# Layer 0's spectrum: Fourier and filter products issued ahead of the next band's mixing product

## The chip, the cores and the metric

The kernel runs on one core of a Trainium2 chip. The metric is device time in microseconds (us), the median of three runs. A core has engines that work through their own queues of instructions in order and meet only by waiting for one another: TensorE (PE in the profile; its weight loads are PEld) multiplies matrices into PSUM, VectorE (DVE), ScalarE (ACT) and GpSimd (POOL) work elementwise, and SyncE (SP) issues most transfers (DMA). TensorE's clock is not constant; the profile shows the share that was granted.

## What is computed

Eight images of 256 channels and 32 x 32 pixels pass two layers. Layer 0 is attention followed by a gated convolution network with a filter in the frequency domain; layer 1 is causal attention over 1024 tokens and a mixture of eight experts. The change is in layer 0, and there in the end of its second half (g1, g2: gammas):

```
x = x + g1 * attention(norm1(x))            # 4 heads, 1024 positions, depthwise 3x3 on v, projection
h = dwconv3(conv1x1(norm2(x), pi_w))        # 256 -> 1024 channels
h = gelu(h[:, :512]) * h[:, 512:]
y = conv1x1(h, po_w)                        # 512 -> 256: the "mixing product"
y = irfft2(rfft2(blocks_8x8(y)) * fft_p)    # filter on each 8x8 block
x = x + g2 * y
```

## The kernel before

**Tiling.** Channels or pixels lie on 128 partitions. An image is two tiles of 128 x 1024. In the spectrum (`spectrum(b)`, L1160) the image is cut into four bands of eight rows. Each band passes three steps. `first(n)` multiplies the band's hidden values with `pow_` (eight matmuls, tile `pz`) and ACT copies the result to `zf`. `second(z)` multiplies with the Fourier matrix (`pf`, one matmul) and VectorE multiplies the result with the filter (`gf`). `third(n, gf)` transforms back (`py`, four matmuls) and VectorE adds it to the image (`t<-py`, two instructions). After the last band the image is stored to `t_d`, and the image three places on is loaded into its buffer, both on SP's queue.

**Buffers.** `pz` comes from a PSUM pool that attention's scores `s` also use. `pf`, `py`, `ms`, `tpy`, `tr`, `rbn` and the projection's `pp` all come from another PSUM pool, `ps_m`, that has two buffers (tag `mm`): each new tile of these waits until whoever reads the buffer's last tile is done. `zf` and `gf` share three buffers in SBUF.

**Stages.** Layer 0 overlaps three images. In stage i (`main_of(i)`, L1240) image i is in attention; image i-1 gets its last projection half (`project`, L995) and its second norm (`norm2`, L1012); image i-2 is in the spectrum. Every step is a generator that is advanced by one yield at a time, and each engine executes its instructions in the order in which the program wrote them (`InOrder`, L61). So the nesting of the generators is the order of the queues. `silent` advances a generator without passing its yields on, `some` passes n of them, and `weave` alternates two generators (L1213 to L1230).

**Beside the main order**, `level` (L461) sets VectorE's convolution taps: after each yield of the main generator it issues taps (`v_conv`, L879: 16 taps `o<-vpad`, eight for each half of the channels; then `hidden`, L1063) until VectorE's planned time has reached the stage's share (`SHARE`) of TensorE's planned time. The planned times are fixed costs per instruction (`TensorCost`, L82; `vector_cost`, L101). The taps `o<-vpad` start from what ACT writes in `v_middle` (L873).

**The second norm** (`rms_norm`, L709) shares the stretch with the spectrum: ACT squares (`sq`), TensorE sums (`ms`), ACT scales (`yr`), TensorE turns (`tpy`), POOL computes seven small steps that end in `r`, TensorE turns back (`tr`), ACT copies (`rT`), TensorE spreads (`rbn`, twice) and VectorE writes `xn`. Between POOL's steps and `tr` stand five empty yields, so that other steps can be woven in.

After the eight stages an ending (L1340 to L1369) runs the spectra of images 6 and 7 beside the first token work of layer 1. For image 7 the mixing products are made ahead (`mix`, L1145), so there `first` is a copy alone.

Of the kernel before, what the change touches and what calls it, by code (L numbers as in the profile page):

```python
# [105 lines left out]
def conv_attn_hybrid_kernel(  # L106
# [34 lines left out]
    def col(name, i=0, n=1):  # L141
        o, w = _VOFF[name]
        assert i + n <= w
        if o >= NVEC0:
            return more[0][:, o - NVEC0 + i : o - NVEC0 + i + n]
        return vec[:, o + i : o + i + n]
# [431 lines left out]
    with ExitStack() as l0:  # L578
# [9 lines left out]
        def load_x(b):  # L588
            t[b] = two.tile([P, KC, N], F32, tag="t", name="t", bufs=3)
            nc.sync.dma_start(t[b], xv[b])  # L590
# [96 lines left out]
        def inside(p, r0, c0, h):  # L687
            o = r0 * (W + 1) + c0
            return p[:, o : o + h * (W + 1)].rearrange("p (h w) -> p h w", w=W + 1)[:, :, :W]
# [7 lines left out]
        def rows(ap):  # L697
            return ap.rearrange("p (h w) -> p h w", w=W)
# [174 lines left out]
        def v_middle(b):  # L873
            o = att[b]["o"] = one.tile([P, KC, N], F32, tag="o", name="o")
            for g in range(KC):
                mid = inside(vpad[g], 1, 1, H)
                act.activation(rows(o[:, g, :]), mid, AF.Identity, bias=pe_o[:, g : g + 1], scale=pe_w[:, g, 4:5])
# [112 lines left out]
        def finish(b):  # L990
            while att[b]["rest"]:
                att[b]["rest"].pop(0)()
                yield 0.4

        def project(b, halves):  # L995
            for h in halves:
                hs = slice(h * HALF, (h + 1) * HALF)
                if h == 0:
                    both = ps_s.tile([P, KC, HALF], F32, tag="s", name="pp")
                    pps = [both[:, g, :] for g in range(KC)]  # L1000
                else:
                    pps = [ps_m.tile([P, HALF], F32, tag="mm", name="pp") for _ in range(KC)]
                for g in range(KC):
                    conv1x1(pps[g], projw, g * P, att[b]["o"], hs)
                    yield 1.7
                for g in range(KC):
                    tb = t[b][:, g, hs]
                    dve.scalar_tensor_tensor(tb, pps[g], proj_o[:, g : g + 1], tb, ALU.add, ALU.add)
# [3 lines left out]
        def norm2(b, gaps=3):  # L1012
            xn2[b] = one.tile([P, KC, N], F32, tag="xn2", name="xn2")
            yield from rms_norm(b, "n2w", xn2[b], gaps)
            ready2[b] = True
# [120 lines left out]
        def gelu_steps(b):  # L1136
            hid = hid_of[b]
            while hid["gelu"] < ng:
                h1 = hid["h"][hid["gelu"]]
                act.activation(h1, h1, AF.Gelu)  # L1140
                hid["gelu"] += 1
                gate(b)
                yield 0.0
# [16 lines left out]
        def spectrum(b):  # L1160

            hid = hid_of[b]["out"]
            nb = H // PS

            def first(n):
                if b in mixed:
                    pz = mixed[b][n // 2][:, n % 2]
                    z = two.tile([P, 2, C], F32, tag="ev", name="zf", bufs=3)
                    act.copy(z, pz)
                    return z  # L1170
                pz = ps_s.tile([P, 2, C], F32, tag="s", name="pz")
                for k in range(2):
                    for g in range(ng):
                        blk = hid[g][:, (2 * n + k) * P : (2 * n + k + 1) * P]
                        pe.matmul(pz[:, k, :], blk, pow_[:, g, :], start=(g == 0), stop=(g == ng - 1))
                z = two.tile([P, 2, C], F32, tag="ev", name="zf", bufs=3)
                act.copy(z, pz)
                return z

            def second(z):  # L1180
                pf = ps_m.tile([P, 2, C], F32, tag="mm", name="pf")
                pe.matmul(pf, dft, z, start=True, stop=True)
                gf = two.tile([P, 2, C], F32, tag="ev", name="gf", bufs=3)
                dve.tensor_mul(gf, pf, filt.unsqueeze(1).to_broadcast([P, 2, C]))
                return gf

            def third(n, gf):
                py = ps_m.tile([P, KC, PS, 2, W // 2], F32, tag="mm", name="py")
                for g in range(KC):
                    for k in range(2):  # L1190
                        pe.matmul(py[:, g, :, k, :], gf[:, k, g * P : (g + 1) * P], idft, start=True, stop=True)
                for g in range(KC):
                    tb = t[b][:, g, n * BAND : (n + 1) * BAND]
                    dve.scalar_tensor_tensor(
                        tb, py[:, g].rearrange("p r k c -> p (r k c)"), col("gam2", g), tb, ALU.mult, ALU.add
                    )

            z, gf = {}, {}
            for n in range(nb + 2):
                if n < nb:  # L1200
                    z[n] = first(n)
                    yield 3.5
                if 1 <= n <= nb:
                    gf[n - 1] = second(z.pop(n - 1))
                    yield 0.9
                if n >= 2:
                    third(n - 2, gf.pop(n - 2))
                    yield 0.9
            nc.sync.dma_start(t_d[b], t[b])
            if b + 3 < B:  # L1210
                load_x(b + 3)

        def weave(main, side, every, rest=True):  # L1213

            for n, us in enumerate(main):
                yield us
                if n % every == every - 1:
                    step = next(side, None)
                    if step is not None:
                        yield step  # L1220
            if rest:
                yield from side

        def some(steps, n):
            for us in itertools.islice(steps, n):
                yield us

        def silent(steps, n=None):
            for _ in itertools.islice(steps, n):
                pass  # L1230

        def none():
            yield from ()

        def later_on(n, steps):
            for _ in range(n):
                yield 0.0
            yield from steps

        def main_of(i):  # L1240

            steps = attend(i)
            if i >= 1:
                if i == 1:
                    second = norm2(i - 1)
                    silent(steps, 1)
                    silent(project(i - 1, (1,)))  # L1250
                    silent(second, 2)
                    v_middle(i)
                    yield from weave(second, steps, 2, rest=False)
                else:
                    mixing, second = spectrum(i - 2), norm2(i - 1, 5)
                    silent(second, 1)
                    silent(mixing, 1)
                    silent(project(i - 1, (1,)))
                    silent(second, 1)
                    v_middle(i)  # L1260
                    yield from some(mixing, 1)
                    yield from some(second, 1)
                    yield from some(mixing, 1)
                    yield from weave(second, mixing, 1, rest=False)
                    yield from weave(mixing, steps, 2, rest=False)
            yield from weave(steps, later_on(3, queries_keys(i + 1)) if 1 <= i < B - 1 else none(), 1)
            gelus = gelu_steps(i - 1) if i >= 1 else none()
            if i + 1 < B:
                stack(i + 1)
                steps, ends = values(i + 1), finish(i)  # L1270
                yield from some(gelus, 2)
                yield from some(steps, 2)
                yield from gelus
                yield from some(ends, 1)
                yield from project(i, (0,))
                yield from some(steps, 2)
                yield from some(ends, 1)
                yield from some(steps, 1)
                yield from ends
                yield from steps  # L1280
            else:
                yield from gelus
                yield from some(finish(i), 1)
                yield from project(i, (0,))
# [62 lines left out]

        norm0, keys0 = first_tokens(early, bank0, bank0)
        mixing, second, ends = spectrum(B - 2), norm2(B - 1), finish(B - 1)
        silent(second, 1)  # L1350
        silent(mixing, 1)
# [718 lines left out]
```

## Time and profile before

| what | value |
|---|---|
| median of three runs | 3064.48 us (3064.29 to 3064.49) |
| the profiled execution's own time | 3065.18 us |
| its span, first to last instruction | 3063.5 us |
| mean granted TensorE clock | 0.979 |
| TensorE busy | 2913.9 us, 95% |
| VectorE busy | 2339.7 us, 76% |
| ScalarE busy | 1621.6 us, 53% |
| layer 0's stages i = 2 to 7, start of the first mixing product in i = 3, 4, 5, 6, 7 | 453.26, 607.12, 760.84, 914.06, 1067.91 us |
| 32 filter products `gf`, one | 685 ns |
| waits of TensorE and its weight loads for `gf` | 24.0 and 30.9 us |

The page of the profile shows one execution. Times of instructions count from the span's start. A row of a timeline gives start, duration, engine, operation, output and inputs with shapes, how many equal instructions it merges, and in brackets how long the engine was idle before it and whose end it waited for. A matmul's end is modelled, since matmuls are pipelined. Where a helper records the instructions, all carry its line (L73), so they are told apart by their tiles.

### The profile page before, as it was taken

Reading aid. Unit: us, or ns where it says so; the run is one execution under the profiler, and the core shown is the slowest. Engines: PE = TensorE matmul, PEld = TensorE weight load, DVE = VectorE, ACT = ScalarE, POOL = GpSimd, SP = SyncE. Lnnn points to the kernel's source line nnn. Section 1 sums busy time; section 2 is a strip of 40 time slices with the busy share of each in tenths; the row PEclk is TensorE's granted clock in tenths of the full one; section 3 lists DMA queues with packets and bytes.
Section 4 is the critical chain, followed back from the end, with each engine's and each line's share of the span. In section 5 each row is a group of like instructions: output and inputs, shape, how many; then the busy total and the mean of one; then the engine's idle time right before and its main releaser. Section 6 shows DMA issues by size and latency. Waiting matters only on the chain.

```text
span 3063.5 us, 41588 instructions
## 1 busy us (share of the span) xinstructions
PE 2913.9 (95%) x16802; PEld 1923.7 (63%) x16802; DVE 2339.7 (76%) x2886; ACT 1621.6 (53%) x2440; POOL 317.1 (10%) x453
## 2 busy tenths in 40 slices
PE   7989999999999989889999999999999999999998
PEld 4644655555555555456666666677777777777775
DVE  2378888888888878776566654688988988888887
ACT  2555554545454535434444443565666666666664
POOL 1011111111111110011222222000000000000000
PEclk8999999999999989999999999999999999999999
DMA  6203030303030301003333311421211251122210
GB/s 196 48 10 83 28 84 28 83 29 83 29 83 29 83 15 35 16 35 128 131 133 122 126 78 69 165 83 49 90 69 69 97 186 69 69 76 90 76 69 29
DMA packets 63856, 234.87 MB, mean 77 GB/s; under 512 B 5590, under 2 KB 13862, under 8 KB 54822
## 3 DMA queue, kind: packets, MB, share of 16 engines
q1 hardware_dynamic: 63654, 232.12, 23.1%
q8 instruction: 134, 2.20, 0.3%
q14 instruction: 68, 0.56, 0.1%
HBM read 140.61 MB, written 91.49 MB: 76 GB/s over the span
## 4 chain that ended last, share of the span: by engine, by line
PE 74%; DVE 14%; ACT 6%; POOL 2%; DMA 2%; issue 2%; SPq 0%; ACTq 0%; DVEq 0%; POOLq 0%
PE pm L73 12%; PE pa L73 11%; PE q L73 11%; PE po L73 9%; PE s L73 6%; PE ph L73 6%; PE pq L73 3%; DVE conv L73 3%; PE sums L73 3%; DVE o L73 3%; DVE x L73 2%; ACT zt_e L73 2%; PE pz L73 2%; PE pv L73 2%; PE pp L73 2%
## 5 line engine op out<-in xcount | busy, mean ns | idle before, releaser
L73 PE MATMUL pa<-ze,w 128*128 128x512 f32 x1488 | 423.2, 393 | 0.0
L73 DVE SCALAR_TENSOR_TENSOR x<-hpad,vec,x 128x1024 f32<-128x1024 f32 x248 | 316.8, 1283 | 68.4 <-ACT x L73 60.9
L73 DVE SCALAR_TENSOR_TENSOR conv<-hpad,vec,conv 128x1024 f32<-128x1024 f32 x256 | 327.4, 1283 | 9.7 <-ACT conv L73 3.6
L73 PEld LDWEIGHTS pa<-ze,w 128*128 128x128 f32 x1488 | 278.4, 188 | 63.3 <-issue 3.3
L73 ACT ACTIVATE h<-pa,bn_o,s1a 128x512 f32<-128x512 f32 x256 | 198.6, 776 | 202.1 <-PE pa L73 202.1
L73 ACT ACTIVATE pT<-s 128x1024 f32<-128x1024 f32 x256 | 247.6, 1024 | 84.4 <-PE s L73 84.3
L73 PE MATMUL po<-pT,vT 128*32 128x256 f32 x4096 | 271.9, 383 | 0.0
L73 PE MATMUL q<-h2p,w 128*128 128x512 f32 x768 | 270.1, 460 | 0.1
L73 DVE SCALAR_TENSOR_TENSOR h<-pa,s1b,h 128x512 f32<-128x512 f32 x256 | 191.6, 748 | 96.4 <-PE pa L73 87.7
L73 PE MATMUL ph<-xn,piw 128*128 128x512 f32 x512 | 238.9, 608 | 13.4 <-ACT vpad L73 6.9
L73 PE MATMUL pm<-h,w 128*128 128x512 f32 x512 | 242.0, 595 | 0.0
L73 PE MATMUL q<-z_first,w 128*128 128x512 f32 x768 | 216.0, 390 | 2.8 <-DVE z_first L73 1.7
L73 PE MATMUL pm<-h1p,w 128*128 128x512 f32 x768 | 216.1, 389 | 0.5 <-DVE h1p L73 0.5
L73 PEld LDWEIGHTS q<-h2p,w 128*128 128x128 f32 x768 | 144.8, 189 | 84.3 <-issue 60.1
L73 DVE SCALAR_TENSOR_TENSOR o<-vpad,pe_w,o 128x1024 f32<-128x1024 f32 x128 | 164.0, 1283 | 26.1 <-ACT o L73 22.9
L73 PE MATMUL s<-qst,kst 128*128 128x256 f32 x1024 | 172.2, 311 | 8.9 <-ACT pT L73 6.3
L73 PEld LDWEIGHTS po<-pT,vT 128*32 128x32 f32 x4096 | 120.1, 110 | 84.4 <-issue 2.8
L73 PEld LDWEIGHTS ph<-xn,piw 128*128 128x128 f32 x512 | 92.3, 192 | 127.5 <-issue 99.5
L73 PEld LDWEIGHTS q<-z_first,w 128*128 128x128 f32 x768 | 143.8, 188 | 34.1 <-DVE z_first L73 2.9
L73 PEld LDWEIGHTS s<-qst,kst 128*128 128x128 f32 x1024 | 136.3, 193 | 45.2 <-issue 28.8
L73 PEld LDWEIGHTS pm<-h1p,w 128*128 128x128 f32 x768 | 144.1, 188 | 31.6 <-DVE h1p L73 0.9
L73 PE MATMUL sums<-pT,ones 128*32 128x256 f32 x2048 | 157.6, 379 | 0.0
(281 smaller groups left out, 5105.8 us busy)
## 6 DMA issues: line engine op xcount, KB each, us to landing
ze<-zd SPq DMA_DIRECT2D x29, 1536.0 KB, 6.4
qst<-part SPq DMA_DIRECT2D x32, 512.0 KB, 9.5
kst<-part SPq DMA_DIRECT2D x32, 512.0 KB, 16.4
te<-ud SPq DMA_DIRECT2D x32, 512.0 KB, 4.1
wd<-parts_w SPq DMA_DIRECT2D x20, 768.0 KB, 3.7
w<-wd SPq DMA_DIRECT2D x20, 768.0 KB, 5.7
zd<-parts SPq DMA_DIRECT2D x14, 1024.0 KB, 3.8
ud<-te SPq DMA_DIRECT2D x18, 512.0 KB, 3.4
```

What stands on the lines that cost most here:

```text
L73: return self._tc.keep_in_program_order(method(*args, **kwargs))
```

## The change

Two edits. In the loop of `spectrum` the second step of band n-1 is issued ahead of the first step of band n, no longer behind it. In `main_of`, for stages i of 2 and up, one more step of the spectrum is issued at once behind the projection and the norm's second step (the `ms` of the first half): with the new order, that is the second step of band 0. The number of steps is the same, so each later step of the spectrum falls one place further on among the norm's steps.

```diff
             z, gf = {}, {}
             for n in range(nb + 2):
+                if 1 <= n <= nb:
+                    gf[n - 1] = second(z.pop(n - 1))
+                    yield 0.9
                 if n < nb:
                     z[n] = first(n)
                     yield 3.5
-                if 1 <= n <= nb:
-                    gf[n - 1] = second(z.pop(n - 1))
-                    yield 0.9
                 if n >= 2:
                     third(n - 2, gf.pop(n - 2))
                     yield 0.9
...
                     silent(mixing, 1)
                     silent(project(i - 1, (1,)))
                     silent(second, 1)
+                    silent(mixing, 1)
                     v_middle(i)
                     yield from some(mixing, 1)
                     yield from some(second, 1)
```

On the queues of TensorE and VectorE in stages 2 to 6 that gives (taps: `o<-vpad`; numbers are bands):

```
TensorE before  pz0 pp ms | pz1 ms pf0 tpy pz2 pf1 py0 pz3 pf2 py1 tr pf3 rbn py2 rbn py3 s
TensorE after   pz0 pp ms | pf0 pz1 ms pf1 tpy pz2 py0 pf2 pz3 py1 pf3 tr py2 rbn py3 rbn s
VectorE before  t<-pp | 8 taps gf0 3 taps gf1 t0 2 taps gf2 1 tap t1 gf3 xn t2 xn t3 2 taps
VectorE after   t<-pp | gf0 8 taps gf1 3 taps t0 gf2 3 taps t1 gf3 t2 xn t3 xn 2 taps
```

In stage 7 the taps are 9, 3, 3 and 1: before, ahead of gf0, gf1, gf2 (with t1 behind it) and gf3; after, ahead of gf1, t0, t1 and t2; none follow. In the ending, `pf0` moves ahead of `rb` and `pz1`, `pf1` ahead of `pp`, and `pz2` and `pz3` come later among the norm's and the tokens' steps (`ms`, `tpt`). ACT's order changes only in the ending.

## The prediction

> **What bounds it now.** I began with the page: busy shares and the clock row.
>
> ```profile
> PE 2913.9 (95%) x16802; PEld 1923.7 (63%) x16802; DVE 2339.7 (76%) x2886; ACT 1621.6 (53%) x2440; POOL 317.1 (10%) x453
> PEclk8999999999999989999999999999999999999999
> ```
>
> TensorE is the bound over the whole, and the chain of waits gives it 74%. The change touches one stretch of each image stage, so I went on to the timeline of TensorE in the stage that starts at 453.26 (i=3: image 1's spectrum runs beside image 2's second norm).
>
> ```profile
> 474.34 2.07 PE L73 MATMUL py<-idft,gf 128*128 128x128 f32 x8 [3.64 <-DVE gf L73]
> 476.20 5.46 PE L73 MATMUL pz<-pow__152,hid 128*128 128x256 f32 x16
> 483.39 0.38 PE L73 MATMUL tr<-ident,r 128*8 128x128 f32 x2
> 489.23 1.19 PE L73 MATMUL s<-qst,kst 128*128 128x256 f32 x8
> ```
>
> Start and duration are in front, the idle time before and its releaser in brackets. TensorE waits 3.64 us for the filter product of band 0, then runs slowly: the third mixing product 5.46 us, against 3.62 for the same one at 466.22. At 489.23 the next attention begins (s). VectorE in the same stretch:
>
> ```profile
> 463.15 10.53 DVE L73 SCALAR_TENSOR_TENSOR o<-vpad,pe_w,o 128x1024 f32<-128x1024 f32 x8 [2.05 <-ACT o L73]
> 473.60 0.68 DVE L73 TENSOR_TENSOR gf<-pf,filt 128x512 f32<-128x512 f32 x1
> 478.03 0.68 DVE L73 TENSOR_TENSOR gf<-pf,filt 128x512 f32<-128x512 f32 x1
> 482.56 0.69 DVE L73 TENSOR_TENSOR gf<-pf,filt 128x512 f32<-128x512 f32 x1 [0.54 <-PE pf L73]
> 500.51 19.65 DVE L73 SCALAR_TENSOR_TENSOR x<-hpad,vec,x 128x1024 f32<-128x1024 f32 x15 [7.61 <-ACT x L73]
> ```
>
> The first gf stands behind eight taps. From 463.15 to 490.3 VectorE has hardly a gap, so it, not the 3.64 us, sets when s starts. Stage i=5 proves it:
>
> ```profile
> 781.92 1.16 PE L73 MATMUL py<-idft,gf 128*128 128x128 f32 x8 [3.64 <-DVE gf L73]
> 782.91 3.62 PE L73 MATMUL pz<-pow__152,hid 128*128 128x256 f32 x16
> 796.18 1.20 PE L73 MATMUL s<-qst,kst 128*128 128x256 f32 x8
> ```
>
> The same wait, but no slow clock: py and pz are issued in 4.5 us, not 7.2, and yet s starts only 0.63 us earlier in its stage (35.34 us after the first pz, against 35.97). From s to the next stage's first pz it is 117.87, 117.88 and 117.87 us in three stages (642.97 to 760.84, 796.18 to 914.06, 950.04 to 1067.91). So a move of s is paid one for one, times six stages. VectorE's own lateness after s is free: it idles 7.61 us before 500.51.
>
> **The change, part by part.** No instruction is added or taken away, and no DMA is moved past another: store and load of t stay behind the last third step on SP's queue, and the last py pair ends about a microsecond earlier. I work on i=3's clock with start-to-start times: tap 1.31 (10.45/8), gf 0.60, t pair 0.79, xn pair 1.34, pz 3.45, py 0.9, pf 0.9; gf to its py 0.75; t to the next py 1.02.
>
> First, pf0 goes from 465.04 to behind ms. Its PSUM buffer is free when the second t<-pp is read (461.1), so it runs 461.2 to 462.2; gf0 runs at 462.3, in the 2.05 us in which VectorE waits for ACT's o. It costs nothing while that cover holds, to 463.15 (0.2 us to spare); without it up to 0.6 us, all taps behind it. That takes 0.60 us out of VectorE's full stretch. TensorE's pz1, ms1, tpy and pz2 all move back 1.0 to 1.3 us, inside what was idle time; pf1 waits about 0.3 us for zf1. ACT's yr and y move back as far, and POOL's 7.6 us chain for r ends near 475.6, well before tr.
>
> Second, py0 no longer waits: its gf is long there, so it runs at 471.0 to 471.9. But the wait isn't gone. In the built order gf1 now stands behind the eight taps (473.6), and pf2 uses the PSUM buffer that gf1 reads: pf2 waits to 474.35, 2.4 us instead of 3.64. Then pz3 to 478.7, py1 (after the t pair of 478.1) 479.1, pf3 480.0 to 480.9.
>
> Third, tr. It waited for gf2; now it takes the buffer of py1, so it waits for the second t pair, and between gf2 and that pair stand three taps, where it was two ahead of gf2 and one behind. VectorE: gf1 473.6, three taps, t0 478.1, gf2 478.9, three taps, t1 483.4, gf3 484.2. tr can't start before 484.3. That is a new wait of 3.4 us, with py2 (needs gf3), rbn, py3 and s queued behind it, each in turn waiting for VectorE. In the old order this tail was fed: tr stood at 483.39.
>
> What follows tr, I take from whole stretches. At full clock (i=5) tr to s is 790.34 to 796.18, 5.84 us; pf3 has left it (1.0), so 4.8, and s starts at 489.1. At half clock I use i=7:
>
> ```profile
> 1099.93 0.38 PE L73 MATMUL tr<-ident,r 128*8 128x128 f32 x2 [1.39 <-DVE gf L73]
> 1100.76 1.74 PE L73 MATMUL pf<-zf,dft 128*128 128x512 f32 x2 [0.45 <-ACT rT L73]
> 1103.47 2.08 PE L73 MATMUL py<-idft,gf 128*128 128x128 f32 x8
> ```
>
> tr to s there is 1099.93 to 1108.31, 8.38, less pf's 1.67: 6.7, so s at 491.0. Here py 2.08 and rbn 1.11, at twice their price, lie in a chain from VectorE to TensorE and back, with nothing beside it. Which of the two is it? The granted clock is the last figure but two of the rows of stretches:
>
> ```profile
> 474.30:478.00 3.70, 3.66 (x13) 3.31 (x14) 3.63 (x3) 0.00 (x0) 0.00 (x0) 0.50 0.00 0
> 1100.70:1104.00 3.30, 3.24 (x8) 1.75 (x9) 2.17 (x3) 1.29 (x2) 0.00 (x0) 0.57 0.00 0
> 1104.00:1108.30 4.30, 4.28 (x20) 3.90 (x19) 3.27 (x6) 0.00 (x0) 0.00 (x0) 0.50 0.00 0
> ```
>
> In five of six stages the 3.64 or 4.84 us wait brought the clock to 0.50; in i=7 waits of 1.39 and 0.45 us so close together did it again, and it stayed through a TensorE busy 4.28 of 4.30 us. The Trainium skill ("TensorE: Matmul & The Clock Gate", Part 1: The HAM clock gate) says that the clock halves after an idle window of about 3.4 us, counted in windows of 3.413 us that run freely; its table "Why this matters for your kernels" asks for no gaps above about 3 us. Read so, a 3.4 us gap fills a window only by luck; the clock would stay, and the sum is the full-clock one below. The row is harsher: a thinly filled window is enough. From 480.9 to 489 the new order holds some 2 us of py and small products in 8 us; some window in it is thinner than i=7's. I take the row, and half clock from somewhere between 482.9 and 486.3. Falling late it spares part of py2, so I use s at 490.9.
>
> Sum. The old s stood at 334.90, 489.23, 642.97, 796.18, 950.04 and 1108.31; shifted by each stage's first pp after pz (302.18, 456.71, 610.58, 764.29, 917.52, 1071.37) onto i=3's clock, that is 489.43, 489.23, 489.10, 488.60, 489.23 and 493.65. For i=2 to 6: 5 x 490.9 less these is +8.9. The half clock then lasts into attention: i=7 needs 6.64 us from s to its ph, i=3 6.16, so 0.5 at least (half clock until 1111.4), and 2.0 if it reaches the dense po products; I take 1.0, nearer to i=7's row, less 0.5 that i=2 pays now: +4.5. In i=7 the old order has it worst (s at 493.65 on this clock); the new one puts tr one tap later, 485.6, and s at 492.3: -1.4. At image 6's spectrum (1218 to 1250) pf0 and pf1 wait some 0.5 and 0.8 us for their zf, but the fourth tpt comes ahead of pz3, 1.4 us earlier, and ACT's zt_e, for which TensorE waits 1.34 us, with it: -1.0 (from -1.5 to +1). Image 7's spectrum keeps its order. Total +11.0, on the profiled 3065.18: 3076.2. The median stands 0.70 below that execution, so 3075.
>
> **Rivals.** The clock holds at 1.00 from 480 on. Then i=2 to 6 give 5 x 489.1, nothing gained, -0.5 for i=2's slow start, i=7 has s at 490.4 (-3.2, and -0.5 behind it), the end -1.0: -5.2, about 3059, not slower. For it speaks i=5, where 1.91 us before tr left the clock alone; against it, that the new gap is nearly twice that and thinly filled behind. It decides at whether tr's wait stays under about 2 us.
>
> The half clock comes too late to matter, or alternates between stages (it can, as i=5 shows): half of the loss, 3064 to 3069.
>
> The half clock lasts deep into attention in all stages, or gf0 comes too late for ACT's cover and pushes all taps: 2.0 behind s and 0.6 ahead, 5 x 1.6 more than forecast: 3083 and above. i=7's return after 3.1 us of s speaks against it.
>
> **Chances.** About 6 us (0.2%) is what a measurement of this kernel can tell from no change. The forecast has 0.72 (3068 to 3082; 0.08 of it within 0.2%), the held clock 0.14 (0.09 faster, 0.05 within), the mixed case 0.08 (0.05 within, 0.03 faster), the long one 0.06. So faster 0.12, within 0.18, slower 0.70. The range leaves out most of the held clock and the upper half of the long case: 3060 to 3084.
>
> **What would show it.** py0 without a wait near 471; pf2 waiting some 2.4 us for gf; tr waiting about 3.4 us for t; the clock at 0.50 from there past s; s some 37.7 us after the first pz. I am wrong if tr waits under 2 us, if the clock reads 1.00 between tr and s, or if s to the next pz isn't 117.9 plus what the clock costs.

## The result, and the profile after

| | kernel before | kernel after |
|---|---|---|
| median, runs on the same chip | 3064.39 us (3062.28 to 3069.32, 6 runs) | 3079.54 us (3074.85 to 3082.54, 6 runs) |
| the profiled execution and its span | 3065.18 and 3063.5 us | 3081.98 and 3080.3 us |
| mean granted TensorE clock | 0.979 | 0.973 |

The ratio of after to before is 1.0044, with a 95% interval of 1.0033 to 1.0056: slower by some 15 us. Executions of one kernel differ by up to 8 us, and the slow ones are those with the lower mean clock (0.973 at 3082.54 us, 0.977 at 3074.85): it falls at other places in each. The first 300 us, which the change doesn't touch, took 4.57 us more in the profiled execution of after than in that of before. So single executions are read by stage here, and totals by medians.

The page of after shows TensorE busy for 17 us more, with the same 16802 instructions: the same work at a slower clock.

```profile
PE 2930.9 (95%) x16802; PEld 1936.0 (63%) x16802; DVE 2341.4 (76%) x2886; ACT 1622.0 (53%) x2440; POOL 315.1 (10%) x453
PEclk8999999999999999999999999999999999999999
```

TensorE's timeline of after in the stage i=3, whose projection product pp starts at 464.44 (it started at 456.71 in before; columns as in the timelines above):

```profile
478.83 1.05 PE L73 MATMUL py<-idft,gf 128*128 128x128 f32 x8
482.15 1.10 PE L73 MATMUL pf<-zf,dft 128*128 128x512 f32 x2 [2.27 <-DVE gf L73]
483.09 3.62 PE L73 MATMUL pz<-pow__152,hid 128*128 128x256 f32 x16
...
487.74 1.02 PE L73 MATMUL pf<-zf,dft 128*128 128x512 f32 x2
491.99 0.58 PE L73 MATMUL tr<-ident,r 128*8 128x128 f32 x2 [3.23 <-DVE t L73]
492.50 2.08 PE L73 MATMUL py<-idft,gf 128*128 128x128 f32 x8
...
498.65 2.08 PE L73 MATMUL s<-qst,kst 128*128 128x256 f32 x8
```

The first py no longer waits and the third pz runs at 3.62 us, where before had 5.46. The saving is given back twice: pf waits 2.27 us for gf, and tr waits 3.23 us for t. VectorE's timeline shows who is late.

```profile
470.88 10.53 DVE L73 SCALAR_TENSOR_TENSOR o<-vpad,pe_w,o 128x1024 f32<-128x1024 f32 x8
481.33 0.68 DVE L73 TENSOR_TENSOR gf<-pf,filt 128x512 f32<-128x512 f32 x1
...
487.14 3.91 DVE L73 SCALAR_TENSOR_TENSOR o<-vpad,pe_w,o 128x1024 f32<-128x1024 f32 x3
490.97 0.87 DVE L73 SCALAR_TENSOR_TENSOR t<-py,vec,t 128x256 f32<-128x256 f32 x2
491.76 0.68 DVE L73 TENSOR_TENSOR gf<-pf,filt 128x512 f32<-128x512 f32 x1
494.61 0.88 DVE L73 SCALAR_TENSOR_TENSOR t<-py,vec,t 128x256 f32<-128x256 f32 x2 [2.17 <-PE py L73]
```

The second gf stands behind eight taps, and the t that tr waits for behind three more. Then the roles turn: at 494.61 VectorE waits 2.17 us for TensorE, whose py now takes 2.08 us instead of 1.16. The rows of stretches (the third figure from the end is the granted clock) show why:

```profile
488.00:490.00 2.00, 0.76 (x2) 0.00 (x0) 1.93 (x3) 0.00 (x0) 0.00 (x0) 1.00 0.00 0
490.00:492.00 2.00, 0.01 (x1) 0.04 (x2) 2.00 (x4) 0.00 (x0) 0.00 (x0) 0.77 0.00 0
492.00:494.00 2.00, 2.00 (x9) 1.58 (x10) 0.44 (x1) 1.37 (x2) 0.00 (x0) 0.50 0.00 0
...
504.00:506.00 2.00, 2.00 (x36) 1.03 (x32) 0.00 (x0) 0.19 (x1) 0.00 (x0) 0.82 0.80 317
```

A mean of 0.77 over the row from 490 means a fall at 491.1, and 0.82 over the row from 504 a return at 504.7. For 13.6 us the clock is halved: through the end of the spectrum and the first 6 us of attention. Stage by stage (us; in brackets, tr's wait):

| stage | pp to s, before | pp to s, after | s to ph, before | s to ph, after | pp to next pp, before | after |
|---|---|---|---|---|---|---|
| i=2 | 32.72 | 34.23 (3.23) | 6.62 | 8.26 | 154.53 | 157.69 |
| i=3 | 32.52 | 34.21 (3.23) | 6.16 | 7.94 | 153.87 | 157.33 |
| i=4 | 32.39 | 34.22 (3.23) | 6.15 | 7.77 | 153.71 | 157.19 |
| i=5 | 31.89 | 33.30 (3.23) | 6.15 | 8.14 | 153.23 | 156.63 |
| i=6 | 32.52 | 34.21 (3.23) | 6.14 | 7.88 | 153.85 | 157.27 |
| i=7 | 36.94 | 35.05 (1.74) | 6.64 | 7.34 | | |

The five stages i=2 to 6 cost 16.92 us: 8.13 ahead of s and 8.79 behind it.

### The profile page after: what moved, and what is told of

Read it like the earlier page. It is cut to its first block, busy times and chain, and to the rows that moved or that the text cites. A ratio compares the mean times of both kernels' runs of the same rounds, so it can differ in the third digit from the quotient of the medians.

```text
span 3080.3 us, 41607 instructions
## 1 busy us (share of the span) xinstructions
PE 2930.9 (95%) x16802; PEld 1936.0 (63%) x16802; DVE 2341.4 (76%) x2886; ACT 1622.0 (53%) x2440; POOL 315.1 (10%) x453
## 4 chain that ended last, share of the span: by engine, by line
PE 74%; DVE 15%; ACT 6%; POOL 2%; issue 2%; DMA 1%; SPq 0%; ACTq 0%; DVEq 0%; POOLq 0%
PE pm L73 13%; PE pa L73 12%; PE q L73 11%; PE po L73 9%; PE s L73 7%; PE ph L73 6%; DVE o L73 3%; PE pq L73 3%; DVE conv L73 3%; PE sums L73 3%; DVE x L73 2%; ACT zt_e L73 2%; PE pv L73 2%; PE pp L73 1%; PE pk L73 1%
## 5 line engine op out<-in xcount | busy, mean ns | idle before, releaser
L73 PE MATMUL s<-qst,kst 128*128 128x256 f32 x1024 | 180.5, 323 | 5.8 <-ACT pT L73 3.3
L73 PEld LDWEIGHTS po<-pT,vT 128*32 128x32 f32 x4096 | 121.3, 111 | 87.8 <-issue 8.2
L73 PEld LDWEIGHTS s<-qst,kst 128*128 128x128 f32 x1024 | 144.8, 205 | 41.6 <-issue 28.6
```

Source lines behind the costliest of these rows:

```text
L73: return self._tc.keep_in_program_order(method(*args, **kwargs))
```

## The experiments

Three theories stood against one another at the start. A, that of the prediction: VectorE's order of work makes TensorE wait ahead of a thin tail, and the wait costs mostly by the clock that it brings down. B: something in TensorE's own order or waits is what costs. C: one of the two edits is the cause by itself. Later texts name their own theories by the same letters. All comparisons are with runs of the kernel before on the same chip, whose medians were 3067.1, 3066.85 and 3065.99 us.

### One edit at a time

The first edit alone leaves the loop as in after and takes the added step out again; the second alone leaves the loop as in before.

The first, against after:

```diff
                     silent(second, 1)
-                    silent(mixing, 1)
                     v_middle(i)
```

The second, against before:

```diff
                     silent(second, 1)
+                    silent(mixing, 1)
                     v_middle(i)
```

> Only the first edit: in the spectrum's loop the second step of band n-1 goes ahead of the first step of band n; nothing more is issued behind the projection. TensorE's order is then pf0 ms pz1 tpy pf1 pz2 py0 pf2 pz3 py1 tr pf3 rbn py2 rbn py3 s. Theory A (VectorE's queue decides: gf1 stands behind eight taps, t1 behind three more, and whatever takes py1's buffer waits for t1): here it is pf3, not tr, that takes py1's buffer, so pf3 waits some 3 to 4 us for t where after has tr wait 3.2, and only what follows pf3 (one product fewer than in after) stands in the exposed tail. s comes about 1 us earlier in its stage than in after (33 us behind pp instead of 34.2), the half clock comes all the same: 3070 us (3064 to 3076). Theory B (the head is what costs: pz1 and pz2 moved back by pf0 and pf1): the head is as in after or worse, so as slow as after, 3080. Theory C (the extra step behind the projection is what costs): as before, 3064.

Measured: 3066.27 us, ratio 1.0002 (0.9994 to 1.0011): as before.

> Only the second edit: the loop keeps its old order, and one more step of the spectrum is issued at once behind the projection (that is pz1 together with pf0, as the loop's second step is reached). TensorE's order is pz1 pf0 ms pz2 tpy pf1 py0 pz3 pf2 py1 pf3 tr py2 rbn py3 rbn s, VectorE's gf0, eleven taps, gf1, t0, two taps, gf2, one tap, t1, gf3. pz1 stands where it stood before. Theory A (VectorE's queue decides): gf0 stands ahead of the taps and has to wait for pf0 behind pz1, so all taps start 2 to 3 us later; gf1 stands behind eleven taps (about 5 us later than in before); pf2 waits for gf1 some 5 us, tr for t1; s is 4 to 6 us later in its stage than in before, the clock halves: 3095 us (3080 to 3110), the slowest of the four kernels. Theory B (the head costs: pz1 and pz2 moved back): here pz1 isn't moved, so about as before, 3064 to 3068. Theory C (each edit costs its share of the loss): between 3066 and 3076.

Measured: 3086.47 us, ratio 1.0064 (1.0050 to 1.0078): the slowest. TensorE's timeline of the first kernel in stage i=3 (pp at 461.57):

```profile
484.88 0.38 PE L73 MATMUL tr<-ident,r 128*8 128x128 f32 x2
485.71 1.13 PE L73 MATMUL pf<-zf,dft 128*128 128x512 f32 x2 [0.45 <-ACT rT L73]
489.04 0.66 PE L73 MATMUL rbn<-rT,pick_n 8*128 8x128 f32 x4 [2.20 <-DVE t L73]
...
492.29 2.08 PE L73 MATMUL py<-idft,gf 128*128 128x128 f32 x8
494.02 2.06 PE L73 MATMUL s<-qst,kst 128*128 128x256 f32 x8
```

And of the second (pp at 464.89):

```profile
479.60 3.62 PE L73 MATMUL pz<-pow__152,hid 128*128 128x256 f32 x16
489.59 2.08 PE L73 MATMUL pf<-zf,dft 128*128 128x512 f32 x2 [6.37 <-DVE gf L73]
```

With the loop's edit alone VectorE is as late as in after (t1 is done 27.4 us behind pp in both), and the wait for t is there too. But it falls on the first rbn, behind tr and the last pf; it is 2.20 us long, and in this stage the half clock comes only with the second rbn and the last py. I had named pf as the one to wait, and 3 to 4 us. s stands 32.4 to 33.3 us behind pp. The five stages lose 4.86 us against before, and i=7 gains 3.9 (s 33.56 behind pp, not 36.94, and 0.50 less behind it): nothing is left over.

With the added step alone pz1 isn't moved back, and yet this kernel is by far the worst: gf0 waits for pf0 behind pz1 and holds up eleven taps, and pf2 waits 6.37 us for gf1. So the head isn't the cause: in the first kernel pz1 is moved back at no cost, in the second it isn't and nothing is saved. Of the two edits the added step is the dear one, some 19 us by itself and some 13 on top of the loop's edit, which alone is worth about nothing. To that extent theory C holds, and its number for the first kernel (3064) was nearer than A's. It doesn't say by what the step costs. That is A's part: how late VectorE's gf1 and t1 are, and who stands behind them.

The 3095 us expected for the second kernel were too dear by 8.5: its half clock comes with the wait for gf1 (pf 2.08 us), is over before the last two py in most stages, and falls again at s (s to ph 6.72 us in i=3).

### The clock, taken out of the wait

Products that nobody reads are put into a wait, so that TensorE is busy there and its order and VectorE's stay as they were.

```diff
+            def fill(m):
+                d = ps_s.tile([P, 2, C], F32, tag="s", name="fill")
+                for _ in range(m):
+                    tc.keep_in_program_order(nc.tensor.matmul(d, dft, piw[:, 0, :HALF], start=True, stop=True))
...
                     gf[n - 1] = second(z.pop(n - 1))
+                    if n == nb and b < B - 2:
+                        fill(3)
```

That is the edit to after; in before it is `n == 2` and `fill(4)`, behind pf1.

> The kernel after, with three products of 128x512 that nobody reads put on TensorE between pf3 and tr in stages 2 to 7, into the idle 3.2 us in which tr waits for t (three of them take 2.6 to 2.8 us at full clock); VectorE's order and tap counts stay. Theory A (the wait costs mostly by the clock that it brings down): tr starts where it did, 27.6 us behind pp, but the granted clock stays near 1.00 to s and behind it; tr to s falls from 6.66 to between 4.8 and 5.8, s to ph from 7.9 to 6.2; 2.6 to 3.6 us a stage less, so 3064 us (3060 to 3067). Theory B (the wait costs as such, the clock is a bystander or falls later anyhow, in the thin chain behind tr): no more than 1 us a stage, 3075 to 3081, or slower where the added products are themselves in the way.

Measured: 3059.69 us (3057.13 to 3066.10), ratio to before 0.9979 (0.9973 to 0.9986), so some 20 us less than after. TensorE's timeline in i=3 (pp at 460.73):

```profile
484.89 2.74 PE L1201 MATMUL fill<-piw,dft 128*128 128x512 f32 x6
488.29 0.38 PE L73 MATMUL tr<-ident,r 128*8 128x128 f32 x2 [0.65 <-DVE t L73]
488.79 1.16 PE L73 MATMUL py<-idft,gf 128*128 128x128 f32 x8
492.88 1.22 PE L73 MATMUL s<-qst,kst 128*128 128x256 f32 x8
```

tr starts where it did, 27.56 us behind pp (27.55 in after). But py takes 1.16 us, tr to s 4.59 instead of 6.66, s to ph 6.17 instead of 7.94. That is 2.07 ahead of s and 1.77 behind it. The clock holds from pp to ph in all of i=2 to 6, and those five stages are 18.5 us shorter than in after. tr still has to come 27.56 us behind pp, for t; that by itself costs next to nothing (s is 32.15 behind pp, 32.52 in before). Theory A holds, at the upper end of the gain that I expected.

> The kernel before, with four products of 128x512 that nobody reads put on TensorE between pf1 and py0 in stages 2 to 7, into the 3.6 us in which py0 waits for gf0; VectorE's order and tap counts stay. In the kernel before, that wait halves the clock in five of six stages and py0 and pz3 take 2.7 us more. Theory A (VectorE's queue sets s, not TensorE's wait): all six stages become like i=5, py0 1.16 and pz3 3.62 us long, yet s comes only about 0.6 us earlier in its stage (31.9 us behind pp instead of 32.5), and i=7 hardly moves: 3061 us (3058 to 3064). Theory B (TensorE's slow stretch is on the path): 2.7 us in each of five stages, 3050.

Measured: 3076.73 us, ratio 1.0037 (1.0023 to 1.0051). Both theories expected a gain, and it is a loss, 9.6 us, two thirds of that of the change. The timeline in i=3 (pp at 458.07):

```profile
475.69 1.16 PE L73 MATMUL py<-idft,gf 128*128 128x128 f32 x8 [0.21 <-DVE gf L73]
476.69 3.62 PE L73 MATMUL pz<-pow__152,hid 128*128 128x256 f32 x16
...
484.12 0.38 PE L73 MATMUL tr<-ident,r 128*8 128x128 f32 x2 [1.97 <-DVE gf L73]
...
486.85 2.07 PE L73 MATMUL py<-idft,gf 128*128 128x128 f32 x8
...
491.69 1.89 PE L73 MATMUL s<-qst,kst 128*128 128x256 f32 x8
```

The first part went as theory A says: py0 and pz3 run at full clock, 2.75 us faster, and tr starts where VectorE lets it (26.05 us behind pp; 26.68 in before). But TensorE, now early, waits 1.97 us for gf2 at tr, and the clock halves behind that: py 2.07, s 33.6 to 34.8 us behind pp. In the kernel before, in i=3, 4 and 6, the half clock fell at py0 and pz3. It stretched work that had to wait for VectorE anyway, filled the later wait, and was over before the tail. It was not only hidden, it kept the tail at full clock. (In i=5 of before there was no early half clock, tr waited 1.91 us, and the clock held even so. Why nearly equal waits differ is shown under "How short a wait still halves the clock".)

### The buffer turn

```diff
             def second(z):
-                pf = ps_m.tile([P, 2, C], F32, tag="mm", name="pf")
+                if b < B - 2:
+                    pf = ps_o.tile([P, 2, C], F32, tag="sm", name="pf")
+                else:
+                    pf = ps_m.tile([P, 2, C], F32, tag="mm", name="pf")
```

> The kernel after, but in stages 2 to 7 pf lies in the PSUM bank of attention's sums (one buffer, idle here), so that pf no longer takes turns with py and tr: tr now gets py0's buffer, whose t is read 4.5 us earlier, and no longer waits for t1. VectorE's order and tap counts stay. Theory A (VectorE's queue decides; the buffer only chooses who stands in front of the wait): tr goes without a wait, 24.3 to 25 us behind pp instead of 27.6, but py2 needs gf3, which stands behind the same three taps and t1, so py2 waits some 3 to 4 us in tr's place; s comes 0.5 to 1.5 us earlier at most (32.7 to 33.7 us behind pp), the half clock comes with the new wait all the same: 3070 to 3077 us. Theory B (the buffer turn is the cause): no long wait is left ahead of s, the clock holds, s comes 2 to 3.5 us earlier and s to ph takes 6.2: 3055 to 3063 us.

Measured: 3061.21 us (3056.58 to 3066.29), ratio 0.9983 (0.9977 to 0.9990). That is theory B's number, not A's, though the clock doesn't hold everywhere, as B had it. The timeline in i=3 (pp at 460.16):

```profile
477.88 2.04 PE L73 MATMUL pf<-zf,dft 128*128 128x512 f32 x2 [2.67 <-DVE gf L73]
479.71 4.23 PE L73 MATMUL pz<-pow__152,hid 128*128 128x256 f32 x16
...
485.64 0.38 PE L73 MATMUL tr<-ident,r 128*8 128x128 f32 x2
486.47 1.16 PE L73 MATMUL py<-idft,gf 128*128 128x128 f32 x8 [0.45 <-ACT rT L73]
...
490.96 1.91 PE L73 MATMUL s<-qst,kst 128*128 128x256 f32 x8
```

tr has no wait, as expected, but py2 doesn't take it over: it waits 0.45 us, for rT. I had py2 wait for gf3, which in the kernel after is no need of data (its operand is gf2) but another turn of the same two buffers, with pf3; the experiment took both turns away. VectorE's order is unchanged, and s still comes 30.8 us behind pp in this stage, 3.4 earlier than in after. So the late t1 costs as much as it does because the shared buffers put tr and py2, and all behind them, in its way: VectorE's order sets how late it is, the buffer turn who waits. The single bank's wait of 2.67 us at pf2 also halved the clock early in i=2, 3 and 4 (pf 2.04 us in i=3), where it is cheap. In i=5 and 6, where it didn't, rbn waits 1.51 us for t and the clock halves in the tail: in i=5 s at 31.25, s to ph 7.65.

### VectorE's taps held back

In stages 2 to 7 the levelling of VectorE's taps runs 10 us behind its plan until the spectrum is done. The number of taps is the same.

```diff
+    held = [0.0]
+
     def level(main, side, share):
...
-            while side is not None and dve.spent - d0 < share * (pe.spent - p0):
+            while side is not None and dve.spent - d0 < share * (pe.spent - p0) - held[0]:
...
                     mixing, second = spectrum(i - 2), norm2(i - 1, 5)
+                    held[0] = 10.0
...
                     yield from weave(second, mixing, 1, rest=False)
+                    held[0] = 0.0
                     yield from weave(mixing, steps, 2, rest=False)
```

> The kernel after, with 10 us of VectorE's planned tap time held back in stages 2 to 7 until the spectrum is done: in the built order no tap stands ahead of gf1, three ahead of t0, three ahead of t1, and ten come behind the last t, where VectorE now idles 7.3 us. The first ph of the next hidden values is issued one s earlier. TensorE has 23.6 us of work between pp and s. Theory A (VectorE's queue is what s waits for): no wait for gf1 or t1 is left; s comes 26 to 29 us behind pp instead of 34.2, the clock is 1.00 to s; 5 to 8 us less in each of six stages and 1.8 behind s: 3035 us (3022 to 3050), well below both kernels. Theory B (VectorE's work is only put off: the taps behind the last t make the first x late and TensorE or ACT waits for them in attention): s comes earlier, but s to the next pp grows by as much, 3060 to 3075. Theory C (the norm's chain over ACT and POOL to tr sets s, not VectorE): s at most 3 us earlier, 3060.

Measured: 3036.40 us (3030.56 to 3038.49), ratio 0.9896 (0.9881 to 0.9911).

> The kernel before with the same 10 us of taps held back: gf0 stands behind no tap, gf1 behind three, gf2 behind three more. Theory A (VectorE's queue is what s waits for; then the order of the spectrum's steps matters little, since no wait is left that it could move): s comes 26 to 29 us behind pp instead of 32.5, py0's wait of 3.6 us and its half clock are gone; 3037 us (3024 to 3052), within 6 us of the kernel after with held taps. Theory B (put-off taps are paid in attention): 3060 to 3075. Theory C (the order of the steps matters by itself): 10 us or more slower than the kernel after with held taps, or as much faster.

Measured: 3030.09 us (3028.34 to 3035.59), ratio 0.9879 (0.9864 to 0.9894). VectorE's timeline of the latter in i=3 (pp at 456.14):

```profile
465.63 0.69 DVE L73 TENSOR_TENSOR gf<-pf,filt 128x512 f32<-128x512 f32 x1 [5.10 <-PE pf L73]
...
484.00 13.04 DVE L73 SCALAR_TENSOR_TENSOR o<-vpad,pe_w,o 128x1024 f32<-128x1024 f32 x10
496.95 20.97 DVE L73 SCALAR_TENSOR_TENSOR x<-hpad,vec,x 128x1024 f32<-128x1024 f32 x16
```

And TensorE's:

```profile
476.51 0.38 PE L73 MATMUL tr<-ident,r 128*8 128x128 f32 x2 [0.29 <-DVE gf L73]
...
482.82 2.05 PE L73 MATMUL s<-qst,kst 128*128 128x256 f32 x8
```

Now VectorE waits for TensorE (5.10 us for pf), tr waits 0.29 us, and s comes 26.2 us behind pp instead of 32.5, in all of i=2 to 6 but one (26.68). Ten taps fill the time in which VectorE idled 7.61 us. From s to the next pp it is 121.8 us, against 121.3 in before, so only 0.5 of the 6.3 us is paid back in attention. Theory A holds for both. With the bind gone, the order of the spectrum's steps matters little: the two medians are 6.3 us apart (four runs each, and the intervals overlap), and the stages i=2 to 6 of the old order are 5.7 us shorter in all (s 26.2 against 26.6 behind pp, and 121.8 against 122.2 to 123.8 from s to the next pp). The version that beats both kernels is therefore the kernel before with its taps held back: 1.2% faster.

### How short a wait still halves the clock

> The kernel after with one unread product of 128x512 instead of three between pf3 and tr in stages 2 to 7: tr's wait falls from 3.23 to about 2.4 us, what follows stays as thin as it was. Theory A1 (a thinly filled stretch of some 3.4 us halves the clock, so it depends on where windows that run freely fall): five waits of the same length give both outcomes, some stages with s 34.2 behind pp and s to ph near 7.9, others 32.2 and 6.2: about half of the 20 us that three products bring, 3066 to 3074. Theory A2 (only an idle stretch near 3 us or more does it, as the length of tr's wait decides): all stages at full clock, 3060 to 3063, as with three products.

Measured: 3061.20 us (3056.71 to 3068.26), ratio 0.9986 (0.9979 to 0.9992).

> The same with two unread products: tr's wait falls to about 1.5 us. Theory A1 (thinly filled stretch): half clock at most in one or two of five stages, 3060 to 3065. Theory A2 (length of the wait): all at full clock, 3060 to 3063. Should the clock halve in most stages, the wait isn't its cause but the thin products behind it: 3073 or more.

Measured: 3059.75 us (3053.74 to 3067.73), ratio 0.9983 (0.9976 to 0.9990).

The times fit A2, the traces refute it. TensorE's timeline with one product, first i=3 (pp at 464.12), then i=4 (pp at 619.42):

```profile
481.83 1.10 PE L73 MATMUL pf<-zf,dft 128*128 128x512 f32 x2 [2.27 <-DVE gf L73]
482.76 3.62 PE L73 MATMUL pz<-pow__152,hid 128*128 128x256 f32 x16
...
491.67 0.38 PE L73 MATMUL tr<-ident,r 128*8 128x128 f32 x2 [2.37 <-DVE t L73]
497.41 2.08 PE L73 MATMUL s<-qst,kst 128*128 128x256 f32 x8
...
637.13 1.59 PE L73 MATMUL pf<-zf,dft 128*128 128x512 f32 x2 [2.27 <-DVE gf L73]
638.52 4.85 PE L73 MATMUL pz<-pow__152,hid 128*128 128x256 f32 x16
...
646.97 0.38 PE L73 MATMUL tr<-ident,r 128*8 128x128 f32 x2 [0.89 <-DVE t L73]
651.57 1.22 PE L73 MATMUL s<-qst,kst 128*128 128x256 f32 x8
```

The same two waits stand in both stages, and the outcome differs. In i=3 pf2's 2.27 us leave the clock alone, tr waits 2.37 us, and the tail is slow: s 33.29 behind pp. In i=4 the same 2.27 us halve it, pf and pz take 1.7 us longer, which eats into tr's wait (0.89), and the tail runs at full clock: s 32.15. i=2 goes the first way, i=5 and 6 the second.

The clock record of the traces shows why. In all eleven traces every change of the granted clock falls on a grid of 3.41 us (to within 0.01 us), and the grid lies elsewhere in each trace. Taken over the cells of this grid, the rows of i=3 and then of i=4 read (the second figure is TensorE's busy time, the third from the end the clock):

```profile
477.17:480.59 3.42, 2.40 (x15) 2.02 (x14) 3.35 (x3) 0.58 (x1) 3.18 (x4) 1.00 0.00 0
480.59:484.00 3.41, 2.17 (x8) 1.59 (x9) 3.37 (x4) 0.00 (x0) 2.12 (x4) 1.00 0.00 0
...
634.19:637.60 3.41, 1.14 (x8) 0.78 (x7) 3.37 (x4) 0.47 (x1) 3.09 (x5) 1.00 0.00 0
637.60:641.01 3.41, 3.41 (x8) 2.36 (x7) 3.34 (x4) 0.00 (x0) 0.64 (x1) 0.50 0.00 0
```

In i=3 the wait is split between two cells, and TensorE is busy for over 2 us of either. In i=4 it lies in one, which is left with 1.14 us, and the clock halves at the cell's end. So it goes in all traces: of the cells at full clock in which TensorE was busy for 0.40 of the time or less, all 121 were followed by a half clock; between 0.40 and 0.60, 47 of 144; above, 43 of over 9100. The limits were chosen by sorting these same cells, so they describe these traces and were tested on no others; why the clock fell behind 43 fuller cells is open. The two stages of before that differed fit as well: in i=3 py0's wait of 3.64 us left 1.03 us of work in one cell (a share of 0.30), and the clock fell; in i=5 it was split, the emptier cell had 1.41 us (0.41), and it held.

With two products tr waits 1.51 us in i=2 and i=4, and the clock halves behind it there as well (the last py 1.88 and 2.04 us); in i=3, 5 and 6 it halves at pf2 and tr has no wait, though in i=3 a second time, in attention (s to ph 8.28). So a wait need not be near 3 us, and it is the place of the half clock, not its being there, that is paid for. A1 had the cause, a thinly filled stretch whose place is a matter of chance; its time was too long because it left out the early half clock at pf2, which takes the tail's away.

## Why the prediction was right

The forecast was 3075 us, slower; measured were 3079.54, and the mechanism was the one forecast. One term was half its size, and that the clock fell in all five stages owes a little to chance (both below). Step by step, in the stage i=3, with the times of after set back by 7.73 us (464.44 less 456.71) to the prediction's clock:

- **The head.** pf0 at 461.24, gf0 at 462.38, the taps at 463.15: as forecast, gf0 is hidden in VectorE's wait for o. The experiment with the added step alone shows what that cover is worth: there VectorE waits 4.33 us for pf0, and that kernel is the slowest.
- **py0 and pf2.** py0 at 471.10 without a wait (forecast 471.0); pf2 waits 2.27 us (2.4), at 474.42.
- **tr.** It waits 3.23 us for t (3.4) and starts at 484.26 (484.3). That the new wait replaces the old one was right, in all five stages.
- **tr to s.** 6.66 us, as taken from i=7; s at 490.92 (490.9). In i=5 it is 5.75, since the clock fell later. Ahead of s the five stages lose 8.13 us, where 8.9 were forecast; the products put into the wait give some 2.07 back in four of the stages and 1.16 in i=5, so the choice of the half clock was right. It falls at 483.35 on this clock (486.27 in i=5), between 482.9 and 486.3 as forecast.
- **The half clock behind s: the term that was mis-sized.** Forecast were 1.0 us per stage, "nearer to i=7's row", less the 0.5 that i=2 paid already, in sum +4.5; measured 8.79, about 1.8 per stage. The row of i=7 in the kernel before had s run for 3.1 us at half clock. In after the half clock lasts 13.6 us in four of the stages and 10.2 in i=5; in i=3 6 of these lie behind s, and both the first s and the first po run in it. The end named as possible, 2.0, was the nearer. The kernel with filled wait confirms the size: 1.77 back behind s in i=3. The difference, 4.3 us, is nearly all by which the result exceeds the forecast: the measured terms here and below add up to +14.9 where +11.0 were forecast, and the medians are 15.15 apart.
- **i=7.** s came 1.89 us earlier (forecast 1.4), and s to ph took 0.70 us more.
- **The ending.** From trs at image 6's spectrum to the ph that follows the spectra it is 32.88 us in before (1217.95 to 1250.83) and 32.06 in after (1236.81 to 1268.87): 0.82 us less, forecast were 1.0. pf0 and pf1 wait 0.49 and 0.68 us for zf (0.5 and 0.8), and the wait of 1.34 us for zt_e is gone. The whole stretch from i=7's ph is 2.26 us shorter, but the rest is chance: ahead of trs the clock was halved for two cells of 3.41 us in this execution of before (from 1145.5 and 1213.8), and not in this one of after.
- **"It, not the 3.64 us, sets when s starts" (it: VectorE).** Right, and shown twice: filled with work, py0's wait brings nothing (and costs 9.6 us of median by the clock that halves later); with taps held back, s comes 6.3 us earlier. One clause of it was too simple: the tail waits for VectorE through the two shared PSUM buffers. With pf in a bank of its own VectorE's order stays and 18 us of median go.
- **"It decides at whether tr's wait stays under about 2 us."** Not so sharp. The clock halved behind waits of 1.51, 1.97 and 2.37 us, and held over ones of 1.91 and 2.27 us. What decides is how little of one cell of 3.41 us is filled, and that depends on where the cell lies.

At the place where the Trainium skill ("TensorE: Matmul & The Clock Gate", Part 1: The HAM clock gate) was weighed, the sum by its rule of an idle window of about 3.4 us gave 3059, the sum by the row 3075. The row was right: in i=3 of after the clock falls at 491.08, when TensorE had been idle for only 2.3 us, at the end of a cell in which it was busy for 1.09 of 3.41 us. In none of the five stages was the cell before the fall idle throughout (shares of 0.13, 0.32, 0.41, 0.55 and 0.35). That its windows have this length and run freely, the clock record shows; that one must be idle throughout, it does not bear out. The fall in all five stages was likely rather than sure: i=4 had the share of 0.41 at which the clock held in i=5 of before, and in i=5 the cell with most of the wait (0.47) left the clock alone; it fell one cell later, behind tr.

Of the six runs of after, the slowest two (3081.98 and 3082.54) come close to the long case, 3083 and above, which had a chance of 0.06: with a term open from 0.5 to 2.0, it deserved more.

## What to carry to other kernels

A wait that disappears at one product can come back at the next that needs the same engine; before moving products about, ask which engine's order the stretch is bound by, and move that. Here ten taps out of the stretch gave 37 us; the products' new order cost 15 while VectorE bound the stretch, and some 6 when it no longer did. Where TensorE must wait, let it wait early, ahead of dense work that has slack, rather than just ahead of a thin chain: the half clock that follows is then hidden. And look at buffer turns as at data: two buffers shared by seven kinds of tiles tie a product to a reader that it has nothing to do with.

## What was not expected of the hardware

- An earlier half clock can be worth having: keeping it away from py0 and pz3 by added work made the kernel 9.6 us slower (3076.73 against 3067.1), since it then came in the tail.
- Eighteen added products, three in each of six stages (2.74 us for the three), made after 20 us faster, and a little faster than before (0.9979). Busy time bought clock.
- The clock halves on a grid of 3.41 us, and a cell need not be empty: in these traces 0.40 of it filled was never enough to hold the clock (121 of 121), while 0.41 could be.
- The half clock after tr's wait lasted 13.6 us in i=3, four cells, though TensorE was busy for 0.99 and 0.92 of the second and third, most of the time with small products and s at half speed. In i=4 of the kernel with one product, where a dense pz followed the wait at once, it lasted one cell, 3.4 us. That small products keep it low is a guess that fits; it wasn't tried.
